# Layer 2's expert mixture cut into two lots, run in pieces beside attention and beside the last loop

## The chip, the cores and the metric

The kernel is one program on one core of a Trainium2 chip. The core has five engines that run side by side, each with its own queue of instructions in a fixed order: TensorE (PE, with its weight loads as PEld), VectorE (DVE), ScalarE (ACT), GpSimd (POOL) and SyncE (SP). SP here only issues DMAs. POOL issues the indirect DMAs (gathers and scatters) and computes a few things that the other engines don't, such as powers. The metric is the device time of one execution in microseconds; the profile's span runs from the first to the last instruction.

## The reference, cut to what matters

The model has four layers on `x` (32 batches, 128 positions, 128 features); each adds a gated cross attention and a gated feed-forward part. Everything is float32. What the change touches is the feed-forward part of layer 2, a mixture of 8 experts of which each token takes the best 2, and the last layer behind it:

```python
# layer 2, feed-forward (x after layer 2's attention, layer-normed)
xn = (x - mu) / jnp.sqrt(var + EPS_LN) * gamma + beta
probs = softmax(xf @ Wg.T + bg)
tp, ti = top_k(probs, 2)
tp = tp / (sum(tp) + 1e-8)
w = sum(one_hot(ti, 8) * tp[..., None], axis=1)
h = gelu(einsum('td,edf->tef', xf, W1) + b1, approximate=False)   # 8 experts, 128 -> 512
y = einsum('tef,edf->ted', h, W2) + b2                             # 512 -> 128
out = x + einsum('ted,te->td', y, w)

# layer 3: depooling of a cumulative patch sum plus a projection of rmsnorm(x), then
def act_quant(x):
    scale = 127.0 / clip(max(abs(x), axis=-1), 1e-5)
    return clip(round(x * scale), -128, 127) / scale
gate = silu(bitlinear(x, w_gate)); up = bitlinear(x, w_up)
x = x + tanh(g) * bitlinear(gate * up, w_down)     # bitlinear quantizes x and ternary weights
```

Layer 1 ends in a mixture of the same kind (8 experts, 128 to 256, Silu times a product, no biases).

## The kernel before

**Groups and stages.** The 32 batches are 8 groups of 4 batches (NG = 8, NB = 4), a group being 128 partitions by 4 by 128. The program has five stages. Stage one (0 to about 1230 us) runs three attentions for all groups: layer 0's, layer 1's cross attention and layer 1's own, with layer 0's multilayer perceptron (`mlp0`) beside them. Then layer 1's mixture (`routes1.run`, to about 1420 us), layer 2's attention (to about 1798 us), layer 2's mixture (`routes2.run`, to about 2003 us), and the last loop (layer 3).

**Turns.** Attention is a row of parts: 4 heads of one group and half of its batches each. In layer 2 a group has 4 parts, so there are 32. `Pipe.run` appends a part (whose maxima are written then) and calls `turn`. A turn t writes, in this order: the finishing and placing of earlier parts, the `weights` (scores again, then Exp, L542) of part t - 4, the `products` (L559) of part t - 5, some entries of `to_move` (scatters and gathers on POOL, 4 a turn in layer 2), one step of `after(g)` of a finished group, and one step of `fill`. `drain` runs the turns that are left (37 turns in all in layer 2), then what is left of the steps. `before`, `after` and the fills are Python generators: each `yield` ends a step.

**Routing and the mixture.** `after(g)` of layer 2 (L1204) adds the attention, takes two layer norms at once (a `pow` on POOL, L247), computes the router's logits `pl`, and calls `Routes.take` (L615): some thirty small DVE instructions that find the two best experts, two products on PE that count the tokens ahead of each one (`pos`, L655 and L656), the slot of each token, and 8 scatters on POOL (L609) that write the group's rows into `by_expert`, a DRAM tensor of blocks of 512 slots per expert. `Routes.run` (L708) then works through 8 + 15 = 23 tiles of 512 slots: 8 first blocks and up to 15 further ones whose place and expert come from a table computed on the chip. A tile loads weights (`w`, 514.5 KB) and rows (`xt`), transposes them (`tp`), scales them by gamma and beta into `xT` (L1227), runs four products `ph` with Gelu (L1233, L1236), four accumulated products `ye` (L746), an added bias (L1240), a transpose back (L753) and a store. Loads are two tiles ahead.

**The last loop.** For each group `fetch` (L771) puts 8 gathers on POOL (L776), `depooled` (L1270) adds the gathered rows (L788), norms (the `pow` of L247) and projects (`px`); `first` (L1287) norms again (the `pow` of L201), quantizes, and runs gate and up products; `second` (L1313) quantizes the 512 wide result, transposes it and runs the down product. `depool[g]`, the patch sums, were computed by `last_layer` (L1107), the fill beside layer 2's attention, and lie in SBUF.

**What sets the order.** The order on each engine is fixed when the program is built. A planner walks the instructions by the order in which they were written, estimates when each is ready, and lets a later one pass where an earlier one isn't ready by its estimate; gathers and scatters keep their order among themselves. In the last loop DVE's instructions of three groups stand mixed for this reason. On the chip the order holds, whatever is late. In stage one, PSUM tiles of `before`, `after` and `mlp0` share one ring of two banks (class `psum`, L854); in layer 2's attention two banks are for `tp`, two for `av`, four for scores.

Of the kernel before, what the change touches and what calls it, by code (L numbers as in the profile page):

```python
# [12 lines left out]
F32 = mybir.dt.float32  # L13
F32R = mybir.dt.float32r
BF = mybir.dt.bfloat16
I32 = mybir.dt.int32
# [9 lines left out]
SLOTS = 512  # L26
CAP = 4096
D = 128
EPS = 1e-5
MORE = (2 * CAP - E) // SLOTS  # L30
BLOCKS = E * CAP // SLOTS + MORE + 1
# [3 lines left out]
class _Cols:  # L35
# [15 lines left out]
    iota_p=1, rev=8, room=8,  # L51
# [10 lines left out]
W3 = _Cols(w_in=128, gate=512, up=512, down=512)  # L62


@with_exitstack
def tile_flamingo_gated(
# [323 lines left out]
    class Pipe:  # L390
# [6 lines left out]
        def __init__(self, moves):  # L397
            self.moves = moves
            self.todo, self.last, self.afters, self.place, self.fill = [], None, [], [[]], []

# [9 lines left out]
        @staticmethod  # L410
        def advance(queue):
            if queue:
                try:
                    next(queue[0])
                except StopIteration:
                    queue.pop(0)

        def turn(self, ahead):
# [18 lines left out]
            self.advance(self.fill)  # L437

        def drain(self):
# [5 lines left out]
            while self.afters:  # L445
                self.advance(self.afters)
            move()
# [139 lines left out]
    class Routes:  # L587
# [3 lines left out]
        def __init__(self, keep, name):  # L591
            self.name = name
            self.slot = keep.tile([P, NG, 2, NB], I32, name=f"slot_{name}")
            self.weight = keep.tile([P, NG, 2, NB], F32, name=f"weight_{name}")
            self.total = keep.tile([P, E], BF, name=f"total_{name}")
            nc.vector.memset(self.total, 0.0)
            self.room = by_expert.pop()
# [17 lines left out]
        def take(self, pool, psum, g, logits, rows, gate, eps):  # L615

            def t(tag):
                return pool.tile([P, NB, E], F32, tag=tag, name=tag)
# [3 lines left out]

            tt = nc.vector.tensor_tensor
# [29 lines left out]
            tt(self.total, before[:, NB - 1], mine[:, NB - 1], ALU.add)  # L653
            pos = psum.tile([P, NB, E], F32, tag="tp", name="pos")
# [3 lines left out]
            tt(at, pos, CST(cst, "room")[:, None, :].to_broadcast([P, NB, E]), ALU.add)  # L658
# [4 lines left out]
            for b in range(NB):  # L663
                for k in range(2):
                    to_move.append(lambda b=b, k=k: self.store(rows[:, b, :], self.slot[:, g, k, b : b + 1]))
# [8 lines left out]
            )  # L674

        def tables(self, pool, psum):


            n = MORE
# [3 lines left out]
            nc.vector.tensor_scalar(nx, cnt, 1.0 / SLOTS, 0.5 - 0.5 / SLOTS, ALU.mult, ALU.add)  # L683
# [17 lines left out]
            nc.vector.tensor_scalar(row[:, 2], row[:, 0], float(CAP // SLOTS), 1.0, ALU.mult, ALU.add)  # L701
# [6 lines left out]
        def run(self, pool, psum, weights, cols, turned, hidden, n_f, finish):  # L708
# [3 lines left out]
            def static(i):  # L712
                return slice(i * (CAP // SLOTS), i * (CAP // SLOTS) + 1), slice(i, i + 1)

            def dynamic(i):
# [5 lines left out]
                    for k, top in ((1, BLOCKS - 1), (0, E - 1))  # L721
                ]
                return bass.ds(vals[0], 1), bass.ds(vals[1], 1)

            def load(i):
# [3 lines left out]
                xt = pool.tile([P, SLOTS // P, D], F32, tag="xt", name="xt", bufs=3)  # L729
# [5 lines left out]

            def first(i):
                block, w, xt = loaded.pop(i)
                xT = pool.tile([P, SLOTS], F32, tag="xT", name="xT")
                turned(xT, flat(transposed(psum, xt)))
                return block, w, hidden(w, xT)  # L740

            def second(block, w, hid):
                y = psum.tile([P, SLOTS], F32, tag="y", name="ye", bufs=1)
# [3 lines left out]
                yT = pool.tile([P, NB, P], F32, tag="yT", name="yT")  # L747
# [3 lines left out]
            def third(block, yT):  # L751
                yt = pool.tile([P, NB, D], F32, tag="yt", name="yt")
                nc.vector.tensor_copy(yt, transposed(psum, yT))  # L753
                ins = nc.sync.dma_start(out=self.room[block].rearrange("o p n -> (o p) n"), in_=flat(yt))
                self.apart(ins, "tiles", "no two tiles share a block")

            n = E + MORE
            loaded = {0: load(0), 1: load(1)}
            hid, done = first(0), None
            table = self.tables(pool, psum)  # L760
            for i in range(n):
# [6 lines left out]
                hid = after  # L768
            third(*done)

        def fetch(self, pool, g):  # L771

            got = pool.tile([P, 2, NB, D], F32, tag="got", name="got")
# [11 lines left out]
        def add(self, g, got):  # L785
            for b in range(NB):
                for k in range(2):
                    nc.vector.scalar_tensor_tensor(  # L788
                        xs[g][:, b, :], got[:, k, b, :], self.weight[:, g, k, b : b + 1], xs[g][:, b, :],
# [27 lines left out]

    def attention_pools(stack, name, bufs, n_weights):
# [24 lines left out]

    by_expert = [dram.tile([BLOCKS, P, SLOTS // P * D], F32, name=f"by_expert{i}") for i in range(2)]
    clear = [(t, n) for t in by_expert[::-1] for n in range(0, BLOCKS, 4)]
    routes1 = Routes(cp, "r1")
    with ExitStack() as stack:
# [6 lines left out]
        class psum:  # L854


            @staticmethod
            def tile(shape, dtype, tag=None, name=None, bufs=None):
                return psum_h.tile(shape, dtype, tag="h", name=name)

# [4 lines left out]
        def layer0():  # L865
# [5 lines left out]
            zeros = mlp.tile([P, SLOTS // P * D], F32, name="zeros")  # L871
            nc.gpsimd.memset(zeros, 0.0)
            def cleared():
                if clear:
                    t, n = clear.pop(0)
                    nc.sync.dma_start(
                        out=t[n : n + 4].rearrange("n p m -> p n m"),
                        in_=zeros[:, None, :].to_broadcast([P, 4, SLOTS // P * D]),
                    )
# [53 lines left out]
            def after(g):  # L933
                add_gated(xs[g], 0, at.pop(g)[-1])
                pipe.fill.append(mlp0(g))
                yield
# [5 lines left out]
        def layer1():  # L942
# [28 lines left out]
            def after(g):  # L971
# [13 lines left out]
                yield  # L985
# [3 lines left out]
        def layer1f():  # L989
# [42 lines left out]
            def after(g):  # L1032
# [20 lines left out]
                routes1.take(pool, psum, g, pl, t, 5, 0.0)  # L1053
                yield
# [414 lines left out]
```

## Time and profile before

| What | us |
|---|---|
| Median of 3 runs (lowest, highest) | 2240.34 (2239.62, 2249.68) |
| The profiled execution, its own time | 2218.45 |
| Its span, first to last instruction | 2216.7 |
| Stage one | 0 to about 1230 |
| Layer 1's mixture | about 1256 to 1420 |
| Layer 2's attention, with the routing of all groups | 1446 to 1798 |
| Layer 2's mixture, last scatter to last store | 1798.6 to 2002.8 |
| Last loop | 2003 to 2217 |
| Busy over the span: PE, DVE, ACT, POOL | 1651.2, 1219.5, 894.8, 643.3 |
| Mean granted PE clock, as a share of full speed | 0.856 |

Durations in what follows come from the profiled execution. A row of the profile's chain of waits gives a start, a length and what held the end of the program back in that time. A row of busy time by stretch gives, for a stretch of the span, the time in which each engine worked (with the number of its instructions), the clock that PE was granted, and what the DMA engines did. A row of the list of waits gives who waited for whom: microseconds in total, number of waits, the longest.

### The profile page before, as it was taken

The page shows a single profiled execution, that of the slowest core. Times are in us where ns is not written, and L with a number is a line of the kernel's source. Part 1 is how long each engine was busy: PE and PEld are TensorE (multiplying, and loading weights), DVE is VectorE, ACT ScalarE, POOL GpSimd, SP SyncE. Part 2 cuts the span into 40 slices and gives each one's busy share as a digit, 9 for nine tenths or more (in the row PEclk, how much of TensorE's full clock was granted, in tenths as well). Part 3 has the DMA queues.
Part 4 walks back from the last instruction along what each step waited for, and adds up shares of the span by engine and source line. Part 5 has one row for each costly group of instructions (what it writes and reads, how often), then busy time and mean ns, then how long its engine had stood idle before and what let it go on. Part 6 is the DMA issues. An engine that isn't in the chain of part 4 may idle for free.

```text
span 2216.7 us, 35517 instructions
## 1 busy us (share of the span) xinstructions
PE 1651.2 (74%) x13624; PEld 1005.0 (45%) x13624; DVE 1219.5 (55%) x3521; ACT 894.8 (40%) x1110; POOL 643.3 (29%) x645
## 2 busy tenths in 40 slices
PE   0699998989999998878777399545656449993444
PEld 0454445456666666555455144233545324441222
DVE  7645455375545577676666333366677421113777
ACT  0376565556777654332333133211112114341334
POOL 5101011010100113345554660254544310004440
PEclk9999999999999999877778599866677569996656
DMA  6574567544232342112121254244344023331110
GB/s 213 147 244 164 181 204 274 162 116 121 86 99 89 99 118 67 51 54 58 51 60 34 79 167 149 94 115 127 99 119 109 21 84 124 118 116 38 29 36 22
DMA packets 162232, 240.46 MB, mean 108 GB/s; under 512 B 20304, under 2 KB 102032, under 8 KB 161808
## 3 DMA queue, kind: packets, MB, share of 16 engines
q1 hardware_dynamic: 153872, 221.42, 32.6%
q0 software_dynamic: 8192, 16.79, 2.7%
q8 instruction: 107, 1.75, 0.3%
q14 instruction: 61, 0.50, 0.1%
HBM read 137.64 MB, written 99.14 MB: 107 GB/s over the span
## 4 chain that ended last, share of the span: by engine, by line
PE 39%; DVE 14%; POOL 13%; issue 7%; ACT 3%; DMA 3%; SPq 0%; POOLq 0%; DVEq 0%; ACTq 0%
PE ye L746 5%; POOL got L776 5%; PE sct L476 4%; PE av L559 4%; POOL by_expert L609 4%; PE ph L1233 4%; PE sc L476 3%; PE ph L918 3%; PE tp L265 3%; DVE mx L507 2%; DMA got<-by_expert,slot_r 2%; PE p L1087 2%; PE p L1085 2%; DVE bst L211 1%; PE tpo L571 1%
## 5 line engine op out<-in xcount | busy, mean ns | idle before, releaser
L542 ACT ACTIVATE w<-sct 128x1024 f32<-128x1024 f32 x288 | 292.6, 1024 | 315.4 <-PE sct L476 312.8
L507 DVE TENSOR_REDUCE mx<-sc 128x8 f32<-128x1024 f32 x160 | 194.6, 1218 | 133.1 <-PE sc L476 132.5
L476 PEld LDWEIGHTS <-stack_q 96*128 96x128 bf16 x2560 | 189.0, 107 | 119.9 <-issue 96.1
L776 POOL DMA_INDIRECT got<-by_expert,slot_r x128 | 126.5, 989 | 354.9 <-issue 354.1
L559 PE MATMUL av<-w,va 128*9 128x128 f32 (+2 forms) x3584 | 200.4, 296 | 37.8 <-POOL w L545 31.7
L512 DVE TENSOR_REDUCE mx<-sc 128x4 f32<-128x1024 f32 x128 | 152.8, 1221 | 130.0 <-PE sc L476 129.5
L476 PE MATMUL sc<-stack_k,stack_q 96*128 96x128 bf16 x1536 | 141.7, 237 | 40.6 <-DVE mx L507 16.5
L476 PE MATMUL sct<-stack_q,stack_k 128*128 128x128 bf16 (+1 forms) x1536 | 140.0, 234 | 21.8 <-DVE mx L507 12.7
L476 PEld LDWEIGHTS <-stack_k 128*128 128x128 bf16 (+1 forms) x1536 | 109.5, 105 | 76.0 <-issue 72.7
L559 PEld LDWEIGHTS av<-w,va 128*9 128x9 f32 (+2 forms) x3584 | 100.2, 94 | 88.4 <-POOL w L545 42.3
L294 POOL CAST hml<-whole 128x512 bf16<-128x512 f32 (+1 forms) x56 | 36.7, 655 | 354.7 <-ACT whole L293 181.5
L746 PE MATMUL ye<-hid,w 128*128 128x512 f32 x276 | 133.3, 593 | 2.3 <-DVE hid L1090 2.3
L201 POOL TENSOR_TENSOR r<-r,m 128x4 f32<-128x4 f32 x56 | 57.1, 1020 | 230.9 <-DVE r L200 219.7
L918 PE MATMUL ph<-h,w 128*128 128x512 f32 x256 | 122.7, 606 | 1.8 <-ACT hn L921 0.9
L918 PE MATMUL ph<-hn,w 128*128 128x512 f32 x256 | 121.2, 604 | 0.7 <-ACT hn L921 0.7
L565 ACT COPY ot<-av 128x512 f32<-128x512 f32 x112 | 65.4, 584 | 128.9 <-PE av L559 90.7
L476 PE MATMUL sc<-stack_l,stack_q 96*128 96x128 bf16 x1024 | 109.8, 237 | 0.0
L1227 DVE TENSOR_SCALAR xT<-tp,col 128x512 f32<-128x512 f32 x23 | 18.6, 809 | 154.9 <-PE tp L265 137.5
L545 POOL TENSOR_SCALAR_AFFINE_SELECT w<-w 128x1024 f32<-128x1024 f32 x64 | 70.3, 1098 | 109.5 <-ACT w L542 109.4
L476 PE MATMUL sct<-stack_q,stack_l 128*128 128x128 bf16 x1024 | 98.8, 234 | 2.7 <-DVE mx L507 2.5
L542 ACT ACT_TABLE_LOAD x72 | 92.4, 1283 | 9.7 <-PE sct L476 8.5
L571 PE MATMUL tpo<-cst,ot 128*128 128x128 f32 x448 | 81.2, 305 | 13.7 <-ACT ot L565 6.6
(289 smaller groups left out, 3345.2 us busy)
## 6 DMA issues: line engine op xcount, KB each, us to landing
by_expert<-zeros SPq DMA_DIRECT2D x40, 1024.0 KB
stack_q<-q SPq DMA_DIRECT2D x96, 288.0 KB
stack_k<-k SPq DMA_DIRECT2D x96, 288.0 KB
k<-hml SPq DMA_DIRECT2D x16, 1152.0 KB
w<-in_e_dram SPq DMA_DIRECT2D x23, 514.5 KB
xt<-by_expert SPq DMA_DIRECT2D x46, 256.0 KB
by_expert<-yt SPq DMA_DIRECT2D x46, 256.0 KB
q<-hml SPq DMA_DIRECT2D x72, 128.0 KB
```

Of the source, the lines that this page charges most:

```text
L476: nc.tensor.matmul(dst[:, h * P : (h + 1) * P], lhsT=stat[rows, 4 * e + h, b], rhs=mov[rows, 4 * e + h, b], start=start and h == e == 0, s ...
L507: nc.vector.tensor_reduce(mx[:, :, b0 : b0 + 2].rearrange("p h b -> p b h"), sc.rearrange("p i (h k) -> p i h k", h=4), AX.X, ALU.max, neg ...
L512: nc.vector.tensor_reduce(mx[:, :, b0], sc.rearrange("p i (h k) -> p h i k", h=4), AX.XY, ALU.max, negate=True,)
L542: nc.scalar.activation(w.rearrange("p i h k -> p i (h k)"), sc, AF.Exp)
L545: nc.gpsimd.affine_select(out=heads, in_=heads, pattern=[[0, 8], [1, P]], compare_op=ALU.is_ge, fill=0.0, base=0, channel_multiplier=-1,)
L559: nc.tensor.matmul(av[32 * h : 32 * h + dv + 1, b * P : (b + 1) * P], lhsT=values[c][:, b, 4 * u + h, :], rhs=w[:, i, h, :], start=c == 0, ...
L571: nc.tensor.transpose(tp[:, b].rearrange("p s r -> p (s r)"), ot[:, b, :], ident)
L609: ins = nc.gpsimd.indirect_dma_start(out=self.rows(), out_offset=bass.IndirectOffsetOnAxis(ap=slots, axis=0), in_=rows, in_offset=None,)
L746: nc.tensor.matmul(y, lhsT=w2[:, f, :], rhs=hid[:, f, :], start=f == 0, stop=f == n_f - 1)
L776: ins = nc.gpsimd.indirect_dma_start(out=got[:, k, b, :], out_offset=None, in_=self.rows(), in_offset=bass.IndirectOffsetOnAxis(ap=self.sl ...
L918: nc.tensor.matmul(ph, lhsT=wt[:, c, f * P : (f + 1) * P], rhs=h[:, c, :], start=c == 0, stop=c == 3)
L1233: nc.tensor.matmul(ph, lhsT=E2(w, "w1")[:, f * P : (f + 1) * P], rhs=xT, start=True, stop=True)
```

## The change

1. A mixture is now a lot of groups with its own slot size: `r1` is layer 1's (groups 0 to 7, 512 slots, as before), layer 2's are `r2` (groups 0 to 4) and `r3` (groups 5 to 7), both with tiles of 256 slots. The number of tiles is 8 + 19 in `r2` and 8 + 11 in `r3`. Each lot has its own DRAM tensor, table and counts.
2. `Routes.run` is a generator that yields after its first loads, after the table and after each tile. Lot `r2` becomes the fill of layer 2's pipe once group 4's routing has finished, two steps a turn. Lot `r3` is stepped by `piece(n)` in the last loop.
3. `take` yields twice, so that routing comes in three steps; the scatters are put on POOL's list in the third. Two `yield`s at the end of other `after`s are gone.
4. In layer 2's attention there is one `av` bank, one `tp` bank, and a ring of two banks that everything else shares, the tiles of `r2` too. In mixture 1 the ring for `p1` and `p3` has three banks instead of four, and `ye` two instead of one.
5. `depool[g]` goes to DRAM and comes back in the last loop. `last_layer` runs at 1.25 steps a turn.
6. In the last loop `fetch` runs two groups ahead of use and issues its gathers at once.
7. The quantizers use three small DVE instructions instead of five, and `fg` one instead of two.

```diff
-SLOTS = 512
-CAP = 4096
-MORE = (2 * CAP - E) // SLOTS
-BLOCKS = E * CAP // SLOTS + MORE + 1
+LOTS = dict(r1=(0, 8, 512), r2=(0, 5, 256), r3=(5, 8, 256))
+def _room(lot):
+    first, end, slots = LOTS[lot]
+    cap = (end - first) * NB * P
+    more = (2 * cap - E) // slots
+    return cap, more, E * cap // slots + more + 1
...
+        def beside(self):
+            self.owed += self.rate
+            while self.owed >= 1:
+                self.owed -= 1
+                self.advance(self.fill)
...
             if ready:
                 self.advance(self.afters)
-            self.advance(self.fill)
+            self.beside()
...
             while self.afters:
                 self.advance(self.afters)
+                self.beside()
             move()
             while self.fill:
                 self.advance(self.fill)
...
             tt(self.total, before[:, NB - 1], mine[:, NB - 1], ALU.add)
+            yield
             pos = psum.tile([P, NB, E], F32, tag="tp", name="pos")
...
             nc.vector.tensor_copy(self.slot[:, g], slot)
-            for b in range(NB):
-                for k in range(2):
-                    to_move.append(lambda b=b, k=k: self.store(rows[:, b, :], self.slot[:, g, k, b : b + 1]))
             den = s("t_d")
...
+            yield
+            for b in range(NB):
+                for k in range(2):
+                    to_move.append(lambda b=b, k=k: self.store(rows[:, b, :], self.slot[:, g, k, b : b + 1]))
...
             loaded = {0: load(0), 1: load(1)}
+            yield
             hid, done = first(0), None
             table = self.tables(pool, psum)
+            yield
             for i in range(n):
                 if i + 2 < n:
                     loaded[i + 2] = load(i + 2)
...
                 hid = after
+                yield
             third(*done)
+            self.done = True
...
-    depool = [tail.tile([P, NB, D], F32, name=f"depool{g}") for g in range(NG)]
+    depool = [dram.tile([P, NB * D], F32, name=f"depool{g}") for g in range(NG)]
...
+    def experts2(routes, pool, psum):
...
+        def gelu(w, xT):
+            hid = pool.tile([P, 4, routes.slots], F32, tag="hid", name="hid")
+            for f in range(0, 4, 2):
+                p = psum.tile([P, 2, routes.slots], F32, tag="h", name="ph")
+                for i in range(2):
+                    nc.tensor.matmul(
+                        p[:, i], lhsT=E2(w, "w1")[:, (f + i) * P : (f + i + 1) * P], rhs=xT, start=True, stop=True
+                    )
+                    nc.scalar.activation(hid[:, f + i, :], p[:, i], AF.Gelu, bias=E2(w, "b1")[:, f + i : f + i + 1])
+            return hid
...
+        return routes.run(pool, psum, e2_d, E2, turned, gelu, 4, finish, 0)
...
-            banks = attention_pools(stack, "a2", 2, 4)
-            pool, psum, _, _ = banks
+            banks = attention_pools(stack, "a2", 1, 4)
+            pool = banks[0]
+            psum_h = stack.enter_context(tc.tile_pool(name="beside_ps", bufs=2, space=PSUM))
+            psum = shared(psum_h)
...
-                    nc.scalar.copy(depool[g], po)
+                    nc.scalar.copy(dep, po)
+                    nc.sync.dma_start(out=depool[g], in_=flat(dep))
...
             pipe.fill.append(last_layer())
+            pipe.rate = 1.25
...
-                routes2.take(pool, psum, g, pl, yn, 6, 1e-8)
-                yield
+                yield from lot(g).take(pool, psum, g, pl, yn, 6, 1e-8)
+                if g + 1 == routes2[1].begin:
+                    move()
+                    while pipe.fill:
+                        pipe.advance(pipe.fill)
+                    e2 = side.enter_context(tc.tile_pool(name="e2", bufs=2, side="right", reuse_waits="tile"))
+                    pipe.fill.append(experts2(routes2[0], e2, psum))
+                    pipe.rate = 2
...
-            routes2.run(pool, psum, e2_d, E2, turned, gelu, 4, finish)
...
+        e2 = stack.enter_context(tc.tile_pool(name="e3", bufs=2))
+        beside = [experts2(routes2[1], e2, shared(psum))]
+        def piece(n):
+            for _ in range(n):
+                Pipe.advance(beside)
...
             nc.vector.tensor_reduce(am, a, AX.X, ALU.max, apply_absolute_value=True)
-            nc.vector.tensor_scalar(am, am, 1e-5, None, ALU.max)
+            inv = pool.tile([P, NB], F32, tag=f"inv_{tag}", name=f"inv_{tag}")
+            nc.vector.tensor_scalar(inv, am, 1e-5, 1.0 / 127.0, ALU.max, ALU.mult)
             sc = pool.tile([P, NB], F32, tag="qs", name="qs")
-            nc.vector.reciprocal(sc, am)
-            nc.vector.tensor_scalar(sc, sc, 127.0, None, ALU.mult)
-            inv = pool.tile([P, NB], F32, tag=f"inv_{tag}", name=f"inv_{tag}")
-            nc.vector.reciprocal(inv, sc)
+            nc.vector.reciprocal(sc, inv)
...
+        def fetch(g, wait=False):
+            while wait and not lot(g).done:
+                piece(1)
+            if g < NG and g not in fetched and lot(g).done:
+                dp = pool.tile([P, NB, D], F32, tag="dp", name="dp", bufs=3)
+                nc.sync.dma_start(out=flat(dp), in_=depool[g])
+                fetched[g] = lot(g).fetch(pool, g, 3), dp
+                move()
...
         def depooled(g):
-            move()
-            routes2.add(g, fetched.pop(g))
+            got, dp = fetched[g]
+            lot(g).add(g, got)
             _, h = layernorm(pool, xs[g], tag=None, again="hx")
-            if g + 1 < NG:
-                fetched[g + 1] = routes2.fetch(pool, g + 1)
+            fetch(g + 1)
+            fetch(g + 2)
...
+        fetch(0)
+        piece(6)
         depooled(0)
-        depooled(1)
         h = first(0)
         for g in range(NG):
-            if g + 2 < NG:
-                depooled(g + 2)
-            after = first(g + 1) if g + 1 < NG else None
+            piece(2)
+            fetch(g + 2)
+            if g + 1 < NG:
+                fetch(g + 1, True)
+                depooled(g + 1)
+                piece(2)
+                after = first(g + 1)
+                piece(1)
             second(g, h)
             h = after
```

## The prediction

> **What bounds the kernel now.** I read the row of slices first (each slice 55.4 us), to see which stage has which engine busy.
>
> ```profile
> PE   0699998989999998878777399545656449993444
> DVE  7645455375545577676666333366677421113777
> POOL 5101011010100113345554660254544310004440
> PEclk9999999999999999877778599866677569996656
> ```
>
> Late in the span, three slices have PE at 9, DVE at 1 and POOL at 0: layer 2's mixture. Before and after them PE is at 3 to 6 on a reduced clock while DVE and POOL work. Busy time by stretch puts numbers on that (columns: stretch, length, PE, weight loads, DVE, ACT, POOL, clock, DMA share, GB/s).
>
> ```profile
> 100.00:700.00 600.00, 560.07 (x5003) 326.67 (x5002) 324.08 (x781) 397.56 (x429) 64.54 (x96) 0.99 0.49 157
> 1712.00:1728.00 16.00, 9.22 (x123) 7.93 (x120) 9.59 (x32) 3.65 (x4) 8.38 (x8) 0.71 0.11 35
> 1728.00:1760.00 32.00, 19.81 (x214) 15.27 (x212) 14.80 (x70) 6.64 (x9) 9.41 (x9) 0.61 0.05 18
> 1760.00:1798.00 38.00, 5.93 (x25) 4.33 (x25) 14.72 (x75) 0.81 (x2) 16.49 (x17) 0.50 0.07 25
> 1810.00:2003.00 193.00, 182.23 (x548) 87.47 (x547) 35.42 (x55) 79.11 (x116) 0.00 (x0) 1.00 0.33 111
> 2003.00:2217.00 214.00, 88.07 (x464) 51.35 (x464) 147.38 (x504) 67.85 (x97) 84.22 (x80) 0.63 0.11 31
> ```
>
> The mixture (from the last scatter at 1798.6 to the last tile's store at 2002.8: 204 us) is PE alone. In the 86 us ahead of it PE works 35.0 us, in the last loop 88 of 214. The chain of waits (start, length, what held it) shows the two different clocks of these stages: a tile every 8.37 us (1842.48 to 1850.85), and a loop group every 22.4.
>
> ```profile
> 1842.48 2.59 PE ye L746 x6
> 1847.41 3.43 PE ph L1233 x8
> 1850.85 2.59 PE ye L746 x6
> ...
> 2089.87 1.25 POOL got L776
> 2091.42 2.57 DMA got<-by_expert,slot_r
> 2098.04 1.81 PE px L1279 x2
> 2112.52 1.25 POOL got L776
> ```
>
> The loop is paced by POOL: eight gathers 1.25 us apart (10 us), landing 2.6, adds and statistics, a `pow`, products, a second `pow`, and only then the next gathers. The waits inside layer 2's attention show one more thing:
>
> ```profile
> POOL by_expert L609 <- DVE slot_r L662: 62.8, 6, 17.2
> PE pos L655 <- DVE t_mine L648: 41.0, 7, 12.0
> ```
>
> PE stood 41 us in seven waits for routing, because `pos` sits in its queue directly behind DVE's whole routing sequence.
>
> **The change, part by part.** *A tile.* In steady state 8 records of `ph` take 3.43 us, so one of 512 columns takes 0.43. Two records make one product; a tile of 256 slots has 16 records of half the columns (16 x 0.215 = 3.44) and half the transposes (1.26 / 2), together 4.1; half the measured period gives 4.2, which I use. There are 8 + 19 = 27 tiles in lot one and 8 + 11 = 19 in lot two: 46 x 4.2 = 193 us of PE, as before (23 x 8.37). Left alone, a small tile takes longer: with two shared banks, PE waits for the turned input (DVE, 809 ns at 512 columns, some 0.5 here, plus 0.3 of latency) and for the last Gelu (687 ns at 512, some 0.46 here): 1.2 us more, 5.4 in all (estimates from these rows).
>
> *Removed:* the 204 us stage.
>
> *Lot one beside attention.* Group 4's routing ends in turn 28: turn t runs weights of part t - 4, and the 25th of the 32 Exp activations starts at 1712.3. Lot one's first input load waits for group 4's eight scatters (8 x 1.26, until 1720.7 in this trace), their landing (2.2) and its own load (3 us): 1726. From there: 27 x 4.2 = 113 of PE, plus attention's own 35.0, which at full clock is 9.22 x 0.71 + 19.81 x 0.61 + 5.93 x 0.50 = 21.6; I take 26. Turns 29 to 36 run 16 tiles, the drain 8, 3 remain. The nearest row for the efficiency is stage one, 100 to 700 us, where a two-bank multilayer fill runs beside attention: 560 of 600, 93%. 139 / 0.93 = 150; the last 11 tiles have almost nothing beside them, 11 x (5.4 - 4.5) = 10. End: 1726 + 160 = 1886, where the old mixture ended at 2003: -117.
>
> *Routing in three pieces* puts a turn between `mine` and `pos`. Of the 41 us, 34 lie ahead of 1712. Bounds: 0 (DVE's sequence is as long, and POOL's scatters come two turns later) to -34. Much of the wait is DVE itself waiting for gathers: -8. In stage one PE waited 8.6 us for the same thing: 0.
>
> *Queues that the pieces pass.* SP: per tile a weight load, an input load, a store (0.33 to 0.45 us of issue each) and two register loads in the dynamic tiles. The first input load blocks SP for some 12 us behind the scatters; behind it stand the rows of the last maxima (L530), needed four turns later (37 turns in some 350 us: 38 us), so it is covered; without cover, 12. POOL: group 4's scatters are flushed at once, so group 5's `pow` can be 5 us late; two tiles of PE work cover it. ACT: Exp and Gelu alternate, as do Silu and Gelu in the loop.
>
> ```profile
> L542 ACT ACT_TABLE_LOAD x72 | 92.4, 1283 | 9.7 <-PE sct L476 8.5
> ```
>
> A load costs 1.28 us here and 0.13 of idle before it. The Trainium skill (ScalarE: Activation LUTs, What ACT_TABLE_LOAD costs) counts 2.66 for each switch, drain included, and its rule is to batch by set, which speaks against this change. About 22 switches fall beside attention: 31 us by the row, 59 by the page. ACT's other work there is 11 + 27 x 5 x 0.46 = 73, so 104 or 132 of 160: not the bound by either; I go by the row.
>
> *The clock.* A second rule against: the skill (TensorE: Matmul & The Clock Gate, A second HAM failure mode) says that cycling through PSUM banks leaves small idle gaps, and that the array's clock then falls back and recovers in turn. At 0.5, as in 1760 to 1798, lot one would take 227 us instead of 113. The row of 100 to 700 has a two-bank ring too, and 0.99: I go by it.
>
> *Last loop.* First loads: 5 us, as at 1800.2 to 1804.7. Until lot two is through (22 advances: 6, then 5 per group, so in g = 3) PE has 19 x 4.2 = 80 and four groups' own work at full clock, 88 x 0.63 / 8 = 7, say 8 each: 112 / 0.9 = 124. Sixteen gathers (20 us) now stand ahead of the first group's second `pow`; PE can take later pieces meanwhile: 4. Last store landing and third stage: 4. Lot two is ready at 137. DVE per group is 147.4 / 8 = 18.4, less five quantizer instructions of 0.16: 17.6. Four groups and a `second` remain, 76; half a `depooled` can come earlier, 70, at 90% 78. The last group's own latency adds 11 (27 us in the final 27, DVE busy 15.9). Sum 226 against 214: +12. Bounds: DVE the only limit, (147.4 - 6.4 + 18) / 0.9 + 16 = 193, -21; the old pace after lot two, 137 + 4 x 22.4 + 27 = 254, +40.
>
> *At nothing:* `depool` through DRAM (eight stores and loads of 256 KB, two groups ahead, DMA share 0.11 in the loop; uncovered, one load, 5 us); one `av` bank (each is read within a turn; uncovered 0.6 per unit, 10 us); in mixture 1 three banks for four, Silu ending before the fourth product wants its bank (0.86 x 3 against 0.86 + 0.9).
>
> **Sum:** -117 - 8 + 12 = -113 on 2216.7, a factor of 0.949. The profiled execution (2218.45) lay 1% below the median of the runs shown, 2240.34; the factor gives **2126 us**.
>
> **The rivals.** *Half of lot two stays in sight.* The loop keeps its POOL order, now with gathers ahead of the second `pow`; for it speaks POOL's place in the chain, against it that fetches run two groups ahead. Half of 19 x 5.4 is 51: -125 + 51 = -74, about 2166.
> *More is hidden.* All 34 us of routing waits go and DVE alone limits the loop: -117 - 34 - 21 = -172 at best, 2067; with half of the extra, about 2097.
> *Lot one only comes after attention*, because the last routing chain keeps PE's order waiting: 1790 + 5 + 27 x 5.4 = 1941, -62 + 12 = -50: about 2190. For it: only 9 turns remain at turn 28.
> *Slower.* PE has one queue in a fixed order. If each tile's inner waits stop attention and the loop instead of being filled by them, the tiles add up: 46 x 5.4 = 248 for 204, +44, about 2284. It decides once less than 44 of 248 us (18%) is covered. For it: `pos` blocked PE by exactly this, up to 12 us at a time. Against: the 93%.
>
> **How the numbers follow.** Likeliest 0.45 (its own range 2095 to 2155), half of lot two 0.20, more hidden 0.12, lot one after attention 0.08, slower 0.15. A measurement here can tell about 0.5% (11 us) from no change. The slower rival puts 0.12 above 2251 and 0.03 into the band, the fourth case 0.02 into it: faster 0.83, same 0.05, slower 0.12. The range 2080 to 2225 leaves out the best part of the second and nearly all of the last, 0.05 + 0.15.
>
> **What would show it.** Right: from about 1726 PE at 9 and a clock of 0.95 or more to some 1880, then a loop near 226 us whose first 130 have PE above 8; `ph` records half as long; `pos` waits under 20 us. Wrong: a clock near 0.5 to 0.7 beside the pieces; PE idle under `xT` or weight loads over 1 us a tile; `pow` late behind gathers with PE idle; lot one's tiles mostly after the last routing.

## The result and the profile after

The changed kernel takes 2249.1 us (median of 20 executions) where the kernel before takes 2240.4 beside it: 1.0043 times as long, 95% interval 1.0026 to 1.0061. The forecast was 2126, with a range up to 2225. One thing has to be known to read the numbers below: the kernel before itself took 2217 us in two of the five sets of experiments and 2237 to 2239 in the other three, so ratios are taken only within a set, and lengths of stages come mostly from runs of one set (the profile shown of before belongs to the first kind, that of after to the second).

The rows of slices of the changed kernel (56.2 us each; engine or clock, one digit per slice):

```profile
PE   0699998889999998878776599265655878767733
DVE  7645455474645676767764333456665422245466
POOL 5101011110100114465554820634443111242140
PEclk9999999999999999978886799566666999878966
```

The three late slices with PE at 9 are gone, and in their place stand seven with PE at 6 to 8, most of them at a clock of 0.8 or more. Busy time by stretch (columns as before: stretch, length, PE, weight loads, DVE, ACT, POOL, clock, DMA share, GB/s): the last turns ahead of the tiles, lot one, the loop until lot two is through, the rest.

```profile
1712.00:1750.00 38.00, 21.54 (x238) 17.52 (x237) 20.00 (x74) 5.50 (x7) 11.22 (x12) 0.65 0.39 103
1750.00:1947.00 197.00, 158.86 (x796) 106.30 (x793) 56.96 (x211) 86.09 (x160) 26.39 (x26) 0.94 0.38 120
1947.00:2131.00 184.00, 133.51 (x583) 88.59 (x583) 89.60 (x294) 106.41 (x165) 50.88 (x49) 0.84 0.31 96
2131.00:2249.00 118.00, 41.06 (x266) 25.22 (x264) 74.47 (x223) 37.62 (x54) 33.34 (x31) 0.66 0.11 29
```

Lot one takes 197 us for 27 tiles, 7.3 each; the loop, counted from lot one's last store, takes 302 where 226 were forecast (184 until lot two is through, 118 after it). The chain of waits shows why a tile is slow even where only its own work is on the path (start, length, what held it):

```profile
1821.55 0.44 PE tpe L766 x2
1821.98 2.00 PE ye L779 x8
...
1824.07 0.48 ACT yT L1126
...
1824.88 0.68 PE ph L1119 x2
...
1825.58 0.48 ACT hid L1122
...
1826.11 0.71 PE ph L1119 x2
...
1826.85 0.48 ACT hid L1122
...
1827.37 0.44 PE tpe L766 x2
```

From `tpe` to `tpe` 5.82 us, and each step waits for the one before it: PE, ACT, PE, ACT in turn, handing the two shared banks to and fro. The forecast had 4.2. More lines, from the waits and groups, matter below: PE's wait for routing ahead of 1745 us, the first gather of the loop waiting for lot one's last tile (the row names a load; the tile's store was issued at 1947.2 us, the gather at 1949.7), and the table loads on ACT between 1914 and 2131 us (ACT's exchange of one table of functions for another).

```profile
PE pos L678 <- DVE t_mine L670: 14.8, 5, 10.5
...
POOL got L814 <- DMA xt<-by_expert_r: 36.7, 1, 36.7
...
L1372 ACT ACT_TABLE_LOAD x14 | 18.0, 1283 | 0.7 <-DVE h L1373 0.5
L1122 ACT ACT_TABLE_LOAD x13 | 16.7, 1283 | 0.2
```

### The profile page after: what moved, and what is told of

Same layout as the page of the kernel before. It is cut to its first block, busy times and chain, and to the rows that moved or that the text cites. A ratio compares the mean times of both kernels' runs of the same rounds, so it can differ in the third digit from the quotient of the medians.

```text
span 2249.5 us, 36705 instructions
## 1 busy us (share of the span) xinstructions
PE 1698.3 (75%) x13995; PEld 1070.5 (48%) x13995; DVE 1223.1 (54%) x3540; ACT 966.3 (43%) x1261; POOL 648.8 (29%) x645
## 4 chain that ended last, share of the span: by engine, by line
PE 37%; DVE 13%; POOL 12%; issue 9%; ACT 6%; DMA 2%; another core or an unknown queue 1%; SPq 0%; POOLq 0%; DVEq 0%; ACTq 0%
PE ye L779 5%; PE av L574 4%; POOL got L814 4%; PE sc L491 3%; PE sct L491 3%; POOL by_expert_r L629 3%; PE ph L960 3%; PE ph L1119 2%; PE p L1146 2%; PE tpe L766 2%; DVE mx L522 2%; PE p L1148 2%; PE tp L272 1%; ACT hid L1122 1%
## 5 line engine op out<-in xcount | busy, mean ns | idle before, releaser
L814 POOL DMA_INDIRECT got<-by_expert_r,slot_r x128 | 126.6, 989 | 187.5 <-issue 138.0
L779 PE MATMUL ye<-hid,w 128*128 128x256 f32 (+1 forms) x460 | 149.6, 459 | 7.6 <-ACT hid L1122 2.8
L1119 PE MATMUL ph<-xT,w 128*128 128x256 f32 x368 | 116.3, 440 | 40.8 <-ACT yT L1126 14.1
L1122 ACT ACTIVATE hid<-ph,w 128x256 f32<-128x256 f32 x184 | 83.7, 474 | 89.2 <-PE ph L1119 75.0
L629 POOL DMA_INDIRECT by_expert_r<-h,slot_r x64 | 62.6, 978 | 147.3 <-DVE slot_r L685 109.7
L1119 PEld LDWEIGHTS ph<-xT,w 128*128 128x128 f32 x368 | 65.9, 207 | 81.8 <-ACT hid L1122 23.6
```

The lines of the kernel that those rows point to most:

```text
L629: ins = nc.gpsimd.indirect_dma_start(out=self.rows(), out_offset=bass.IndirectOffsetOnAxis(ap=slots, axis=0), in_=rows, in_offset=None,)
L779: nc.tensor.matmul(y, lhsT=w2[:, f, :], rhs=hid[:, f, :], start=f == 0, stop=f == n_f - 1)
L814: ins = nc.gpsimd.indirect_dma_start(out=got[:, k, b, :], out_offset=None, in_=self.rows(), in_offset=bass.IndirectOffsetOnAxis(ap=self.sl ...
L1119: nc.tensor.matmul(p[:, i], lhsT=E2(w, "w1")[:, (f + i) * P : (f + i + 1) * P], rhs=xT, start=True, stop=True)
L1122: nc.scalar.activation(hid[:, f + i, :], p[:, i], AF.Gelu, bias=E2(w, "b1")[:, f + i : f + i + 1])
```

## The experiments

"Loop" is the time from the loop's first gather to the end of the span. The second column is the kernel before, measured beside the run.

| run | before, us | ratio to before (95%) | loop, us |
|---|---|---|---|
| changed kernel again | 2239 | 1.0061 (1.0035 to 1.0087) | 298.8 |
| lot one behind attention | 2217 | 1.0140 (1.0084 to 1.0195) | 296.2 |
| lot two's pieces ahead of the loop | 2217 | 1.0115 (1.0067 to 1.0163) | 300.2 |
| one function in the loop | 2217 | 0.9982 (0.9968 to 0.9997) | 277.4 |
| lot two in its own stage | 2239 | 1.0086 (1.0058 to 1.0114) | 236.1 |
| the same, in a ring of two banks | 2217 | 1.0222 (1.0185 to 1.0259) | 231.8 |
| the same, with the lead of before | 2239 | 1.0024 (0.9992 to 1.0055) | 218.3 |
| the same, four gate and up banks | 2239 | 1.0032 (1.0002 to 1.0062) | 224.2 |
| changed kernel with the lead | 2217 | 1.0080 (1.0058 to 1.0103) | 299.6 |
| the same, one function | 2217 | 0.9957 (0.9933 to 0.9981) | 272.3 |
| before: small tiles | 2217 | 0.9951 (0.9937 to 0.9964) | 209.4 |
| before: routing in pieces | 2239 | 0.9917 (0.9895 to 0.9939) | 209.7 |
| before: quantizers and fetches | 2239 | 1.0000 (0.9981 to 1.0019) | 210.2 |
| before: fewer banks in attention | 2239 | 0.9961 (0.9936 to 0.9985) | 211.7 |
| before: small tiles, routing | 2239 | 0.9873 (0.9814 to 0.9932) | 210.5 |
| before: these, two result banks | 2237 | 0.9789 (0.9757 to 0.9821) | 210.8 |

**The changed kernel again**, as the comparison for its set.

> The changed kernel itself, unaltered, as the comparison on the same chip: 1.002 to 1.007 times the kernel before.

As expected; its trace begins layer 2 seven microseconds later than the one shown and agrees with it within 3 us in each stage after that.

**What lot one beside attention hides.** Its pieces wait until attention has drained:

```
-                    pipe.rate = 2
+                    pipe.rate = 0
```

> Changed kernel with the fill rate 0 instead of 2 once lot one is queued: its pieces all come after the attention's drain, the rest is as it was. Shows the attention of the changed kernel without tiles beside it, and 27 small tiles alone. Theory TILE PRICE: 27 x 5.8 = 157 us alone too. Rival, NEIGHBOURS (a tile is dear only because attention's work stands between): 27 x 4.2 to 27 x 4.6, 113 to 125 us. Theory SLOWER ATTENTION (one av bank and the shared ring of two make the attention itself longer): last scatter near 1825 us instead of 1798.6; rival: the tiles slow it, then near 1800. Total with 1800 and 157: 1962 for the end of lot one instead of 1947, 2264 us; with 1825 and 157: 2289 us; with 1800 and 120: 2227 us.

Attention alone ends with its last scatter at 1790.9 us, so neither the bank cuts nor anything else made it longer (the theory of a slower attention falls). The stretches of this run, attention's end and lot one alone:

```profile
1750.00:1791.00 41.00, 19.05 (x97) 12.15 (x98) 21.82 (x109) 6.60 (x13) 21.68 (x22) 0.58 0.12 37
1791.00:1941.00 150.00, 124.14 (x508) 80.72 (x506) 24.20 (x50) 57.57 (x126) 0.89 (x1) 1.00 0.46 146
```

The tiles come every 5.83 us with nothing beside them. 41 + 150 = 191 us here, 197 with both at once: they add up. Attention's last scatter comes at 1912 us beside the tiles, so attention waits for them. From layer 2's first weights (ACT's table load ahead of them) to the loop's first gather it is 481.5 us in this run and 477.4 in the next one, whose lot one lies beside attention: 4 us are hidden out of 157.

The two also differ in table loads: beside attention Exp and Gelu alternate, 13 loads between 1752 and 1887 us, where this run has one at 1776. The chain of waits of the changed kernel between 1750 and 1947 us passes through seven of them, 9 us in all:

```profile
1752.16 1.28 ACT L1122
...
1754.32 1.28 ACT L557
...
1758.81 1.28 ACT L557
...
1761.14 1.28 ACT L1122
...
1778.60 1.28 ACT L1122
...
1833.43 1.28 ACT L1122
...
1887.37 1.28 ACT L1122
```

No run has one function beside attention, so what they cost there isn't measured.

**Lot two's pieces ahead of the loop**, by the order of the program alone:

```
-        piece(6)
+        piece(100)
```

> Changed kernel with all of lot two's pieces before the first group of the last loop: nothing of it is mixed with the loop. 19 tiles of 5.8 us = 110 plus 5 for the first loads, then the loop alone; Silu and Gelu never alternate. If TABLES is right, mixing costs about as much as it hides: loop alone 195 to 210 us, together 310 to 325 instead of 302, total 2257 to 2272 us, or even less than the changed kernel. If mixing hides as the prediction said (some 75 of 110 us), total 2310 to 2325 us.

This parted nothing: the planner orders instructions by its own estimates, and it mixed the tiles with the first groups again (gathers from 1943 us on, the last tile's store at 2124; loop 300 as before). The run says nothing on mixing, but much on how little the written order binds. It also stands nearest to the changed kernel among the runs beside a kernel before of 2217 us, and there it is 1.2% slower (0.7 to 1.6): the 0.4% of the result was measured where the kernel before took 2240.

**Lot two in a stage of its own**, with two banks each for turning, products and results (the last argument also gives it a third buffer for inputs and a second for results in SBUF):

```
+    with ExitStack() as stack:
+        e2, psum = mlp_pools(stack, "f2")
+        for _ in experts2(routes2[1], e2, psum, 1):
+            pass
...
-        beside = [experts2(routes2[1], e2, shared(psum))]
+        beside = []
```

> Changed kernel with lot two in a stage of its own between attention and the last loop, with two banks each for turning, products and results, the loop then without pieces. Unlike moving the pieces ahead within the loop (there the planner mixed the instructions again), this really parts them. From lot one's end to the end of the changed kernel: 301.8 us. Theory ADDS (a mixed tile hides nothing: the loop's own 190 plus 19 x 5.83 = 111): apart 19 x 4.76 + 8 = 98 plus a loop of 190, 288, the total 14 us below the changed kernel. Theory HIDES (mixing does hide some 40 us, which table loads and the shared banks eat up elsewhere): 98 plus a loop of 214, 312 to 317, 10 to 15 us above the changed kernel.

Neither theory had the loop right: without a single piece in it, it takes 236 us, 26 more than in the kernel before (the next run has the same loop and takes 231.8, 22 more). So mixing does hide time (19 tiles add 298.8 - 236.1 = 63, not 19 x 5.83 = 111), and something else in the new loop costs. The total's interval overlaps with the changed kernel's. The tiles come every 4.26 us here (15 periods from 1937.2 to 2001.1).

**The ring.** The same stage with all of a tile in one ring of two banks:

```
-        for _ in experts2(routes2[1], e2, psum, 1):
+        for _ in experts2(routes2[1], e2, shared(psum), 1):
```

> The changed kernel with lot two in its own stage as before, but with everything of its tiles in one shared ring of two banks, as beside attention and the loop. With two banks for each purpose the tiles came every 4.4 us (15 periods in 67 us). Theory RING (the two shared banks make the tile dear): 5.8 us a tile, the stage 19 x 1.4 = 27 us longer. Rival (neighbours and the clock make it dear): 4.4 to 4.8, under 8 us longer.

15 tiles in 87.5 us, 5.83 each, against 4.26 (the expectation's 4.4 counted one period too few). The time between attention's last scatter and the first gather grows from 107.8 to 135.5: 27.7 us, as the ring theory said; against the two other runs with this stage, further down, it is 24. First the stage with its own banks, then with the ring:

```profile
1935.00:2001.00 66.00, 63.12 (x313) 50.00 (x312) 14.42 (x32) 33.40 (x77) 0.00 (x0) 1.00 0.56 180
```

```profile
1939.00:2027.00 88.00, 73.67 (x304) 48.06 (x302) 14.56 (x31) 34.51 (x76) 0.00 (x0) 1.00 0.41 132
```

Nothing but the banks differs in the program: PE is busy for 96% of the stretch in the one and 84% in the other, at the same clock, and fifteen tiles take 64 us in the one and 87 in the other.

**The new loop's 22 to 26 us.** Two suspects, each undone in the kernel with lot two apart: the written order, in which a group is depooled directly ahead of its own quantizers instead of one group earlier, and the two banks for gate and up products where four stood.

```
         depooled(0)
+        depooled(1)
...
-            fetch(g + 2)
+            if g + 2 < NG:
+                depooled(g + 2)
...
-                fetch(g + 1, True)
-                depooled(g + 1)
```

> The changed kernel with lot two in its own stage (its loop without pieces took 236 us, where the loop of the kernel before takes 210), and the loop's written order of before restored: two groups depooled ahead, then group g + 2 before the quantizers of g + 1. Theory LEAD (the changed order gives a group's chain of gathers, powers and quantizers only one group of room): 27 us per group fall to 22 to 23.5, loop 205 to 215 us, total 20 to 30 us below the kernel with lot two apart, 0.996 to 1.000 of the kernel before. Rival GATE BANKS (two banks for gate and up where four stood): no change, under 5 us.

```
-                pg = psum.tile([P, 512], F32, tag="g", name="pg")
+                pg = psum.tile([P, 512], F32, tag="g", name="pg", bufs=4)
```

(and `pu` likewise)

> The changed kernel with lot two in its own stage, and four banks in turn for the gate and up products of the loop as in the kernel before, the written order of the changed kernel kept. Theory GATE BANKS: loop 236 falls to 210 to 218 us, total 18 to 26 us lower. Theory LEAD: under 8 us.

Both count, neither as much as its theory said: the lead 14 to 18 us (236.1 or 231.8 to 218.3), the banks 8 to 12 (to 224.2). Both at once were not tried. Neither was a line of the prediction. The same lead in the whole changed kernel, with its pieces:

> The changed kernel, all its pieces mixed as they are, with the loop's written order of before: two groups depooled ahead. Alone that took 18 us off the loop without pieces (236 to 218). Theory LEAD holds in the mixed loop too: 299 falls to 280 to 285 us, ratio 0.997 to 0.999. Rival (the pieces fill those waits already, and lot two is needed one group earlier): 0 to 6 us.

Nothing: 299.6 us. The rival is right in its number; of its reasons the trace shows the second, lot two is now needed a group earlier (no Silu runs between 2088.5 and 2170.6 us: lot two's last store is at 2121.0, the next group's gathers begin at 2123.8).

**Silu and Gelu.** Gelu in the place of Silu in the loop, first in the changed kernel, then with the lead:

```
-                nc.scalar.activation(sil, pg, AF.Silu, scale=fg[:, 0, b : b + 1])
+                nc.scalar.activation(sil, pg, AF.Gelu, scale=fg[:, 0, b : b + 1])
```

> Changed kernel with Gelu in place of Silu in the last loop's gate product (so the output differs: this leaves out the true gate function). No table of functions has to be exchanged in the loop any more. Theory TABLES (the alternation of Silu and Gelu on ACT is what makes the loop long): 27 loads of 1.28 us and the turn-arounds behind them go, the loop falls from 302 us by 35 to 60, total 2190 to 2215 us. Theory TILE PRICE (a 256-slot tile simply costs PE 5.8 us instead of 4.2, and PE paces the loop's first half): ACT is not on the path, under 10 us, total 2240 to 2250.

> As the run before, with Gelu in place of Silu in the loop (leaves out the true gate function). Theory TABLES as an own term: 18 to 25 us below the run before, as 300 fell to 277 without the lead. Rival (table loads only fill the waits that the missing lead made): under 8 us.

23 us off the loop against the run with lot two's pieces ahead, beside which it was measured (300.2 to 277.4), and 27 with the lead (299.6 to 272.3); less than the 35 to 60 of the first expectation, much more than its rival's 10. The stretch until lot two is through in the two runs with the lead, with both functions and with one, and the loads in the loop of the first, all but one of them in this stretch (the second has none in its loop):

```profile
1935.00:2121.00 186.00, 136.86 (x591) 95.89 (x589) 89.96 (x295) 101.64 (x162) 50.77 (x49) 0.84 0.31 95
```

```profile
1937.00:2095.00 158.00, 120.32 (x590) 87.61 (x589) 88.22 (x295) 70.33 (x138) 50.64 (x49) 0.90 0.36 112
```

```profile
L1372 ACT ACT_TABLE_LOAD x13 | 16.7, 1283 | 0.2
L1122 ACT ACT_TABLE_LOAD x12 | 15.4, 1283 | 0.2
```

ACT was busy for only 102 of 186 us, and yet taking 31 us of loads from it shortened the stretch by 28. They stand between a product and the activation that reads its bank; that the held bank is what PE then waits for is argued. The granted clock also rises, from 0.84 to 0.90, and no run parts the two.

**Parts alone, on the kernel before.** Tiles of 256 slots in its mixture, one lot, in its own stage with four banks for products (`SMALL = 256` for `SLOTS` in the second `Routes`):

> Kernel before with tiles of 256 slots in layer 2's mixture (39 tiles instead of 23), its own ring of four banks, nothing else changed. Measures the price of a small tile where nothing stands beside it and banks are plenty. The prediction's price, half of 8.37: 39 x 4.2 = 164 + 11 of start and end = 175 us for the stage of 204, total about 2211 us. Theory TILE PRICE, weight loads and fixed costs don't halve: 39 x 5.0 to 39 x 5.8 = 195 to 226 + 11, total 2242 to 2273 us; if the ring of two banks makes part of the 5.8, the lower of these.

39 tiles every 4.76 us; 199.6 us from last scatter to first gather instead of 208.4, and 0.5% faster. The price lies between the two expectations: the tile is 13% dearer than the prediction's 4.2 here, and 39% in the ring. Routing in three pieces:

> Kernel before with routing in three pieces (both layers), nothing else. Prediction's term: -8 us, bounds 0 to -34, in layer 2; 0 in layer 1. In the changed kernel layer 2's first weights come 9 us earlier (1467.9 for 1476.6 us); if layer 1's routing pieces did that, -9 more, -17 us in all. Rival: the later scatters of each group make the next stage start later, 0 or a loss of up to 5 us.

-0.83%, some 19 us, in the set where before took 2239. From the first weights to the last scatter 323 us against 340 in the run below, which is the kernel before up to its loop. But `pos` itself was waited for 37 us in the one and 41 in the other, so the prediction's reason for the gain isn't what the trace shows. And the profile of before, whose execution took 2218, has 321 us for the same stretch without the pieces; lot one behind attention, which has them and was measured where before took 2217, has 324. So the pieces gain 17 us in the one kind of set and nothing that shows in the other. What the gain rests on stays open. The quantizers and fetches:

> Kernel before with the changed kernel's shorter quantizers and its fetch up to two groups ahead in the last loop, nothing else. Prediction's view: DVE paces the loop once gathers come early, 17.6 us of DVE per group at 90% plus 16 and 11: 183 to 195 us instead of 214, total -20 to -30 us. Rival (POOL's order paces it, and eight or sixteen gathers now stand ahead of a group's second power): 205 to 214 us, total 0 to -9 us.

Nothing, the rival's end: 23 us per group as before, though DVE has less to do. Fewer banks in attention (`attention_pools(stack, "a2", 1, 4)` and a shared ring for the rest):

> Kernel before with the banks of the changed kernel in layer 2's attention: one bank for values, one for turned parts, and one ring of two for all that stands beside it. Theory SLOWER ATTENTION (the cuts stretch it): 8 to 20 us longer, ratio 1.004 to 1.009. Rival (each bank is read within a turn, the prediction's 0 with 10 us uncovered): 0 to 3 us.

0.4% faster, which neither expected, in a set where before took 2239. Where it took 2217, attention with these cuts and the routing pieces ends as soon after its first weights as in the profile of before (324 us and 321). So nothing shows that these cuts cost anything, as predicted, and that they gain isn't shown for both kinds of set.

**A version that beats both.** Small tiles with routing in pieces, then with a second bank for a tile's results:

```
-                y = psum.tile([P, n_s], F32, tag="y", name="ye", bufs=1)
+                y = psum.tile([P, n_s], F32, tag="y", name="ye", bufs=2)
```

> A version that may beat both: the kernel before with 256-slot tiles in layer 2's mixture (alone 0.9951) and routing in three pieces in both layers (alone 0.9917), nothing beside anything. If the two add: 0.987, some 29 us below before. If the routing pieces' gain was a matter of how stalls fell in that set of runs: 0.993 to 0.996.

> The kernel before with 256-slot tiles in layer 2's mixture, routing in three pieces (the pair gave 0.9873) and a second bank for the tiles' results. Theory RING (the banks that a tile waits for set its price): 4.4 instead of 4.7 us a tile, 39 tiles, 12 to 14 us less, ratio 0.980 to 0.984. Rival (the rest is landing of the loads): no change, 0.986 to 0.989.

The gains add (0.9873), and the bank brings the tile to 4.33 us and the kernel to 2187.8 us against 2236.8 beside it, 2.1% faster (1.8 to 2.4), with no mixture run beside another stage. The version was measured only where before took 2237 and more, and the 0.8% of its routing showed only there. Its mixture:

```profile
1797.00:1962.00 165.00, 155.90 (x758) 127.51 (x757) 36.19 (x88) 85.19 (x190) 0.00 (x0) 0.98 0.56 179
```

## Why the prediction was wrong

The run of before with new quantizers and the changed kernel run again are of one set. Times in us; the first of them is the kernel before up to the loop, and its loop measured the same as before's.

| stretch | before | changed | measured | predicted |
|---|---|---|---|---|
| start to layer 2's first weights | 1479.8 | 1475.1 | -5 | 0 |
| first weights to first gather of the loop | 547.7 | 478.7 | -69 | -125 |
| loop | 210.2 | 298.8 | +89 | +12 |
| sum | | | +15 | -113 |

**A tile of 4.2 us** is the step that failed first. As PE's work it was right: in a stage with banks enough the records of 256 columns start 0.216 us apart, half of the 0.43 of 512, and the tiles come every 4.26 to 4.33 us. But I gave the 5.4 us of a tile that waits for its two shared banks only to the 11 tiles left alone, and took for granted that elsewhere attention fills the waits. The ring makes it 5.83: 27 x 1.63 = 44 us in lot one, 24 to 28 measured in lot two in a stage of its own.

**93% of PE beside attention** failed next. Stage one was the nearest row for two banks, but not for how much PE does between two waits: there a fill step is four accumulated products, eight records of 512 columns or 3.4 us at 0.43 each; here a step is two records of 256 (0.7 us) or eight (2.0 us), as the chain shows. Measured, 4 us of lot one are hidden; the sum (1886 instead of 1917 for 118 us placed behind attention) counted on 31. The missing 27 and the 44 make 71, and the larger gain from routing (17 us in this set for 8) gives 9 back: 62 for the 56 missing. (Where before takes 2217, its stretch is 529.5 in the profile and 477.4 in lot two's pieces ahead: 73 missing, with no gain from routing 79.) That attention and tiles add up is shown; why is in part open. Step size is argued. Two more things stand in the traces: the seven table loads on the chain, 9 us, and the start. The first input is scaled 21.1 us after the 25th weights in all ten traces with tiles beside attention, where the sum had its load landed after 13.7.

**The loop, 77 us off.** Ring 24 to 28 (measured in lot two's own stage; in the mixed loop it wasn't tried apart) and table loads 23 to 27 are measured. The base is the third: I let DVE pace the loop at 90% once gathers come early, which meant 183 to 195 us without tiles, and the quantizers and fetches alone left it at 210 (15 to 27). Together 62 to 82, and 77 are missing. In a loop without pieces the lost lead and the two gate banks would have cost 22 to 26; I didn't list either. With the pieces the lead was worth nothing, and what the banks cost there wasn't tried.

**Table loads.** I priced them beside attention only, 22 for 31 us, and set them aside because ACT's busy time came to 104 of 160 us; the loop's loads I named and gave no price. Beside attention there were 13, and ACT was busy for 86 of 197 us; in the loop there were 27. The busy share was the wrong test: ACT is busy for 106 of 184 us until lot two is through, and yet 25 loads cost 27 us of path in the kernel with the lead, 1.1 each. The Trainium skill (ScalarE: Activation LUTs, What ACT_TABLE_LOAD costs) has 2.66 for a switch, which would have been 66; the trace's 1.28 is nearer, but the page's rule to batch by set (Table sets: the hidden batching unit) was the warning to price, and I answered it with a busy share.

**The clock** held in the ring: 1.00 in lot two's stage with PE idle for 16% of it, in gaps of up to 0.7 us, so the fall of the clock that the Trainium skill describes for a kernel that cycles through banks (TensorE: Matmul & The Clock Gate, A second HAM failure mode) didn't occur there. Beside attention it was 0.94. In the loop the sum had full clock until lot two is through, and that failed: 0.84. PE was busy there for 133.5 us, and 133.5 x 0.84 = 112 is just the work that the sum had at full clock (my estimate from this row). Whether the lower clock lengthened the path or only followed from PE's waits, no run parts.

**Routing** -8: 17 to 19 us measured where before takes 2239, nothing where it takes 2217, the reason open. PE's waits at `pos` did fall in the changed kernel, from 41 us in all to 15 ahead of 1745 us; where before takes 2217, the stage with the pieces is no shorter for it (23 us of waits at `pos` in lot one behind attention). **Bank cuts in attention and `depool` at nothing:** the cuts cost nothing that shows; `depool` was not tried alone. Lot one's first input was scaled at 1750.7 instead of landing by 1726: 7 us are the 21.1 for 13.7 above, and 17 are the 25th weights, at 1729.5 instead of 1712.3. These 17 are mostly a difference between sets: the 25th weights come at 1712.6 to 1726.0 in the runs with tiles beside attention where before takes 2217, and beside the changed kernel's 1735.8 in the set of the table the kernel before has 1730.8.

**The rivals.** The slower one had the mechanism: PE's fixed order stops attention for a tile's inner waits, and the tiles add up, with 5.4 for 5.83 and a threshold of 18% hidden for a tie. Now 46 x 5.83 = 268; hidden are 4 in lot one and 111 - 63 = 48 in lot two, 19%, against a loop that is itself 22 to 26 dearer and a routing that is cheaper in this set, and the total lands near a tie. That it is so near is in part luck, since these two have nothing to do with the rival's argument. I gave it 0.15 on the strength of the 93%.

## What to carry to other kernels

Before moving a stage beside another, work out the chain of one of its units with the banks that it will have there, PE and ACT in turn, and take that as its price unless the work beside it is shown to be long enough per step and to stand in the right place of PE's queue. A function of another table set can cost its loads on the chain of waits, however idle ACT is on the whole: 1.1 us for each load of 1.28 in this loop. First make the stage shorter where it stands: the same small tiles in their own stage with enough banks, and the routing split, gave 2.1% where the interleaving lost 0.4% (both beside a kernel before of 2237 us or more).

## What was not expected of the hardware

In the three sets where the kernel before took 2237 us and more, and in the trace of the changed kernel, there are waits whose releaser is no instruction or queue of the kernel ("remote"); none of the traces of the other two sets has one, nor has the profile of before. In the run with new quantizers:

```profile
ACT w L542 <- remote: 33.8, 4, 13.8
...
DVE mx L507 <- remote: 13.6, 2, 8.4
```

In the longest of these PE had ended the products some 11 us before ACT and DVE went on together. In size they would do for the 1% between the sets, but that they make it isn't shown: with routing in pieces ACT still has 28.8 us of them, and the stage is 17 us shorter. What they are, no run shows.

Records of 256 columns start 0.216 us apart, those of 512 0.429: half, with the same 128 x 128 weight load of 0.19 us for each, which is nearly as long as the small record. (The 1.99 us of eight `ye` in the chain also holds a slower start of the second, after 0.32 us, and the end of the last.) So halving the tile cost PE next to nothing here, and 39 small tiles have 9984 slots where 23 large ones have 11776.
